# Two last sequences routed by weight to all experts, and squares of the norms written to another tile, in a Mamba and mixture-of-experts kernel

## The chip, the cores and the metric

The kernel runs on one core of one Trainium2 chip. The metric is the device time of one execution, in microseconds (us). Before the change three runs took 5281.4, 5284.5 and 5313.1 us; the median is 5284.5 us. One execution was profiled: it took 5285.57 us, of which 5283.4 us lie between its first and its last instruction (its span).

Five engines have instruction queues of their own and run them in order: TensorE (PE; PEld is its weight load), VectorE (DVE), ScalarE (ACT), GpSimd (POOL) and SyncE (SP), which here only issues DMA transfers.

## What is computed

32 sequences of 512 tokens by 256 channels, all float32, go through one block:

```
h = x + mamba(layernorm(x))                 # in_proj, causal conv of 4 taps, scan over 16 states, gate, out_proj
m = layernorm(h); m = gelu(m @ w1 + b1) @ w2 + b2
x1 = layernorm(x + (h + m))
scores = softmax(x1 @ gate.T)               # 8 experts
weights, idx = top_k(scores, 2)
y_e = (silu(x1 @ wg[e].T) * (x1 @ wu[e].T)) @ wd[e].T        # inner width 128
ffn = sum over the 2 chosen e of weights * y_e  +  the shared expert's y
out = layernorm(x1 + ffn)
```

A token needs only its two experts. A kernel can gather the rows of each expert, or compute every expert for every token and give those not chosen the weight 0.

## The kernel before

Everything about one sequence lies in tiles of 128 partitions: four blocks of 128 tokens (`NC` = 4), or 256 channels as two blocks (`KM` = 2). Four generators describe the work:

- `front(b)`: loads x, takes sums by an ACT copy with an accumulator, `layernorm` (squares on ACT, `nm`, `rs`, `mr` as small POOL operations), transposes through PSUM to `xnT`, in_proj, convolution, the step sizes `dt` and `dt*x`, which go to DRAM (`sdt`, `sdx`) and come back spread over partitions (`dtr`, `dxr`).
- `scan(b)`: 32 steps. In each, `u = dxr * B` (DVE, a few on POOL), two exponentials `pda` on ACT (into two PSUM tiles) and two scans on DVE, then `u = u * C` on POOL, and a PE matmul with `gather` that sums states into `py`. At the end of each quarter `py` is gated by `pz` into `xc`.
- `finish(b)` = `middle(b)` (out_proj `po`, `layernorm`, transposes to `hT`, the MLP `pm`, gelu `hid`) and `back(b)` (`layernorm`, transposes to `x1T`, gate logits `pg`, `route`, the shared expert). `route` finds two experts and their weights per token, counts positions by matmuls, and `back` scatters each token's row twice to `rows_in` in DRAM, 8 indirect DMAs on POOL. The shared expert's result plus x1 goes to DRAM as `sums`.
- `experts(g)`: for a group of sequences, tables on DVE, then blocks of 128 sorted rows, two by two: load rows `xb` and weights `wb` (384 KB), transpose (`pt`, `xT`), gate and up (`pe`), `tb`, `hb`, down (`pd`), `yb` to `rows_out` in DRAM. Then per sequence 8 indirect DMAs on POOL gather `yg`; each is multiplied by a diagonal of weights `dg` into `pc`, added to `sums` as `at`, normalised and written out.

Groups: six of 4 sequences, three of 2, and two of 1 (sequences 30 and 31). A group of n sequences has 8n + 7 blocks: 39, 23 or 15, in all 333. While `scan(b)` runs, `finish(b-1)`, `front(b+1)` and the group's `experts` are called in turn, at set speeds (`N_FRONT`, `N_FINISH`); experts of sequences 28 and 29 run beside `scan(31)`. After the last scan come `finish(31)`, the experts of 30 and those of 31. For the last group of all, `SPACE` gives the tiles of `experts` the buffers that the scan no longer needs.

The order on each engine is not the order of these calls. `Book` records every call; `arrange` (a list scheduler with a cost for each kind of instruction) then picks, among the calls whose inputs and buffers are ready first, the one recorded earliest, and the kernel is emitted in that order. A tile with a tag and `bufs` buffers waits for a buffer of that tag; with one buffer free, only the next tile of the tag in recorded order may take it. `hold` keeps a call behind the one before it, in that order only. Where the scheduler sees PE idle for over 0.6 us while a `py` tile is open, it puts fillers there: matmuls of `zeros` with `ident` into `py`, which add nothing. Each recorded matmul shows as two instructions in the trace (3922 fillers are recorded, 7844 ran).

Squares of a norm (their values are not used, only the sum from the accumulator) go to a tile with the tag `sq`, which has one buffer for all norms of all generators, a new tile for each block of tokens.

Of the kernel before, what the change touches and what calls it, by code (L numbers as in the profile page):

```python
# [122 lines left out]
class Book:  # L123
# [19 lines left out]
    def hold(self):  # L143


        self.held[len(self.calls)] = len(self.calls) - 1
# [213 lines left out]
def kernel(  # L360
# [140 lines left out]
    def totals(nm):  # L501

        return small.tile([P, NC], F32, tag="tot", name=f"tot_{nm}")

    def layernorm(src, tot, nm):

        nm16 = small.tile([P, NC], F32, tag="nm", name=f"nm_{nm}")
        rs = small.tile([P, NC], F32, tag="rs", name=f"rs_{nm}")
        mr = small.tile([P, NC], F32, tag="mr", name=f"mr_{nm}")
        root = DM**0.5  # L510

        nc.gpsimd.tensor_scalar(nm16, tot, -1.0 / (DM * root), 1.0, ALU.mult, ALU.mult)
# [58 lines left out]
    def front(b, got):  # L571
# [107 lines left out]
    dtrs, dxrs, bps, us, bcs = {}, {}, {}, {}, {}  # L679

# [66 lines left out]
    def scan(b):  # L747
# [37 lines left out]
        for k in range(b * per, (b + 1) * per):  # L785
# [33 lines left out]
    def middle(b, ys, got):  # L819
# [9 lines left out]
        mr, rs = layernorm(h, tot, f"b{b}")  # L829
        yield  # L830
        hT = work.tile([P, KM, S], F32, tag="mT", name=f"hT_{b}", bufs=1)
# [72 lines left out]
    def route(b, pg):  # L904
# [3 lines left out]
        g, i0 = place[b]  # L908
# [17 lines left out]
        if i0 == 0:  # L926
# [3 lines left out]
        weight = weights[g][:, i0]  # L930
# [24 lines left out]
        nc.vector.tensor_tensor(both, one, oh, ALU.add)  # L955

# [29 lines left out]
    def back(b, h, tot):  # L986
        mr, rs = layernorm(h, tot, f"c{b}")
        yield
        acc = h
        x1T = work.tile([P, KM, S], F32, tag="mT", name=f"x1T_{b}", bufs=1)  # L990
# [33 lines left out]
        nc.vector.scalar_tensor_tensor(t, pu, 0.5, th, ALU.mult, ALU.mult)  # L1024
        r = rows_in[place[b][0] % 2]
# [22 lines left out]

    def experts(g):

        nb = n_blocks(g)

        last = g == len(groups) - 1

        def space(tag, bufs):
            return SPACE[tag] if last and tag in SPACE else dict(tag=tag, bufs=bufs)

# [92 lines left out]
        for k in range(pairs):  # L1150
# [7 lines left out]
            xT = work.tile([P, KM, 2, P], F32, name=f"xT_{g}_{k}", **space("xT", 2))  # L1158
# [14 lines left out]
            th = work.tile([P, 2, P], F32, name=f"tb_{g}_{k}", **space("tb", 1))  # L1173
            he = work.tile([P, 2, P], F32, name=f"hb_{g}_{k}", **space("hb", 1))
# [10 lines left out]
            yb = work.tile([P, 2, DM], F32, name=f"yb_{g}_{k}", **space("yb", 2))  # L1185
# [7 lines left out]
        for i0, b in enumerate(groups[g]):  # L1193
            at = work.tile([P, NC, DM], F32, tag="at", name=f"at_{b}", bufs=1)
            nc.sync.dma_start(at, sums.pop(b))
            for c0 in range(0, NC, 2):
                po = ps.tile([P, 2, DM], F32, tag="tk", name=f"pc_{b}_{c0}", bufs=4)
                for c in range(c0, c0 + 2):
                    for k in range(TOPK):
                        i = (i0 * TOPK + k) * NC + c  # L1200
                        y = work.tile([P, DM], F32, name=f"yg_{b}_{k}_{c}", **space("yg", 3))
# [8 lines left out]
                        dg = work.tile([P, P], F32, name=f"dg_{b}_{k}_{c}", **space("dg", 2))  # L1210
# [46 lines left out]
    for b in range(NB):  # L1257
# [23 lines left out]
        ending, n_ending = finish(b, fronts[b][1]), N_FINISH  # L1281
# [18 lines left out]
HID_BUFS = 4  # L1300

SPACE = dict(
    wb=dict(tag="u", bufs=U_BUFS),
    xb=dict(tag="dtr", bufs=DT_BUFS),
    xT=dict(tag="bc0", bufs=NG + 1),
    yb=dict(tag="bc1", bufs=NG + 1),
    yg=dict(tag="bc0", bufs=NG + 1),
    dg=dict(tag="dtr", bufs=DT_BUFS),
    tb=dict(tag="hid", bufs=HID_BUFS),
    hb=dict(tag="th", bufs=2),  # L1310
)
# [88 lines left out]
```

## Time and profile before

| what | us |
|---|---|
| median of three runs (all: 5281.4, 5284.5, 5313.1) | 5284.5 |
| profiled execution | 5285.57 |
| its span | 5283.4 |
| PE busy, fillers included | 4831.1 (91%) |
| fillers alone (`py<-ident,zeros`, 7844) | 1002.5 |
| DVE busy | 4165.3 (79%) |
| POOL busy | 3927.9 (74%) |
| ACT busy | 3686.4 (70%) |
| indirect DMAs on POOL, scatter and gather, 256 each | 266.3 and 269.4 |
| end of the last gate of scan 31, from the span's start | 5095.7 |
| from there to the end of the span | 187.7 |

Busy time is the union of an engine's instructions; waiting, branching and issuing of DMAs are not in it. The rows of the profile name instructions by the tiles that they write and read, with numbers left out. Line numbers are of little use here, because nearly every call is made in one place of `Book`; groups are told apart by tiles.

### The profile page before, as it was taken

What the parts mean: (1) busy time and instruction counts of PE and PEld (TensorE: products, weight loads), DVE (VectorE), ACT (ScalarE), POOL (GpSimd) and SP (SyncE); (2) the same over time, 40 slices, a digit from 0 to 9 for tenths busy, and PEclk for the clock granted to TensorE, in tenths of its full rate; (3) what the DMA queues carried; (4) which work ended last, traced back from release to release, by engine and by line L of the source; (5) the groups of instructions that cost most, each with busy time, mean ns of one, the idle gap of its engine ahead of it and who ended that gap; (6) DMA issues with size and microseconds to landing.
All of it is one profiled execution on the core that took longest, in us unless ns stands there. A gap on an engine that the chain in (4) does not pass through costs nothing. (4 is left out here: it accounts for less than half of the span.)

```text
span 5283.4 us, 83847 instructions
## 1 busy us (share of the span) xinstructions
PE 4831.1 (91%) x27968; PEld 2843.5 (54%) x27968; DVE 4165.3 (79%) x5630; ACT 3686.4 (70%) x6812; POOL 3927.9 (74%) x2662
## 2 busy tenths in 40 slices
PE   7999999999999999999999998999998999999885
PEld 3655555555555555555555555555455555655664
DVE  3888888887888878888778887888787768788741
ACT  6677667777767776777777676787776767677542
POOL 3788777778877797777877788777886777777642
PEclk9999999999999999999999999999999999999997
DMA  5753335444454544554444444545356445454534
GB/s 174 242 177 116 109 112 180 150 155 133 144 168 160 162 131 134 168 164 160 146 142 149 162 151 149 170 150 165 124 166 214 157 132 186 143 169 135 170 111 153
DMA packets 521088, 816.68 MB, mean 155 GB/s; under 512 B 49472, under 2 KB 251072, under 8 KB 520656
## 3 DMA queue, kind: packets, MB, share of 16 engines
q1 hardware_dynamic: 493632, 741.95, 43.3%
q0 software_dynamic: 24576, 67.14, 3.9%
q8 instruction: 221, 3.62, 0.3%
q10 hardware_dynamic: 2448, 2.24, 0.1%
q14 instruction: 211, 1.73, 0.1%
HBM read 597.36 MB, written 213.78 MB: 154 GB/s over the span
## 5 line engine op out<-in xcount | busy, mean ns | idle before, releaser
L96 POOL TENSOR_TENSOR u<-u,bc 128x1024 f32<-128x1024 f32 x1024 | 2413.1, 2363 | 597.4 <-DVE u L96 439.3
L96 DVE TENSOR_TENSOR_SCAN u<-pda,u 128x512 f32<-128x512 f32 x2048 | 2400.3, 1209 | 216.1 <-ACT pda L96 187.4
L96 ACT ACTIVATE pda<-dtr,a_neg 128x512 f32<-128x512 f32 x2048 | 1383.6, 686 | 454.1 <-DVE u L96 442.0
L96 DVE TENSOR_TENSOR u<-dxr,bp 128x1024 f32<-128x1024 f32 x896 | 1076.5, 1207 | 191.5 <-PE py L96 77.5
L429 PEld LDWEIGHTS py<-ident,zeros 128*128 128x128 f32 x7844 | 967.8, 197 | 141.0 <-issue 128.4
L429 PE MATMUL py<-ident,zeros 128*128 128x128 f32 x7844 | 1002.5, 281 | 0.0
L96 PE MATMUL py<-u,gather 128*32 128x512 f32 x4096 | 650.9, 623 | 40.6 <-POOL u L96 40.3
L96 PE MATMUL pin<-xpad,taps 32*32 32x512 f32 x4096 | 465.7, 590 | 10.5 <-POOL xpad L96 7.6
L96 PEld LDWEIGHTS pe<-xT,wb 128*128 128x128 f32 x2664 | 358.5, 208 | 171.2 <-DMA wb<-in_w_e_dram 55.9
L96 PE MATMUL pe<-xT,wb 128*128 128x128 f32 x2664 | 386.9, 297 | 69.1 <-DMA wb<-in_w_e_dram 55.1
L96 POOL DMA_INDIRECT rows_in<-h,idx x256 | 266.3, 1040 | 184.6 <-DMA rows_in<-h,idx 99.7
L96 ACT COPY bp<-bc 128x512 f32<-128x512 f32 x512 | 299.6, 585 | 119.7 <-DVE u L96 104.0
L96 POOL DMA_INDIRECT yg<-rows_out,got x256 | 269.4, 1052 | 141.6 <-issue 67.5
L96 ACT ACT_TABLE_LOAD x279 | 358.0, 1283 | 14.4 <-DMA in_sb<-in_in_w_dram 7.9
L96 POOL TENSOR_TENSOR u<-dxr,bc 128x1024 f32<-128x1024 f32 x128 | 302.3, 2362 | 51.2 <-DMA dxr<-sdx 41.0
L96 PE MATMUL po<-out_sb,xc 128*128 128x256 f32 x1024 | 272.9, 402 | 26.8 <-DVE xc L96 26.0
L96 PEld LDWEIGHTS pin<-xpad,taps 32*32 32x32 f32 x4096 | 119.5, 104 | 313.1 <-issue 273.5
L96 PE MATMUL pz<-xnT,in_sb 128*128 128x512 f32 x512 | 267.8, 635 | 10.7 <-DVE h L96 9.0
L96 PEld LDWEIGHTS po<-out_sb,xc 128*128 128x128 f32 x1024 | 187.9, 196 | 139.1 <-DVE xc L96 54.1
L96 PE MATMUL pm<-w_sb,hid 128*128 128x256 f32 x1024 | 255.8, 390 | 1.0 <-ACT hid L96 0.5
L96 PE MATMUL pin<-xnT,in_sb 128*128 128x512 f32 x512 | 252.2, 612 | 3.3 <-DVE h L96 1.8
L96 PEld LDWEIGHTS py<-u,gather 128*32 128x32 f32 x4096 | 100.3, 110 | 278.8 <-POOL u L96 127.7
(168 smaller groups left out, 6388.9 us busy)
## 6 DMA issues: line engine op xcount, KB each, us to landing
dtr<-sdt SPq DMA_DIRECT2D x512, 256.0 KB, 3.6
dxr<-sdx SPq DMA_DIRECT2D x512, 256.0 KB, 3.4
wb<-in_w_e_dram SPq DMA_DIRECT2D x333, 384.0 KB, 3.8
bc<-rows SPq DMA_DIRECT2D x256, 256.0 KB, 3.4
xb<-rows_in SPq DMA_DIRECT2D x333, 128.0 KB, 2.5
rows_out<-yb SPq DMA_DIRECT2D x161, 256.0 KB, 4.4
sdt<-dt SPq DMA_DIRECT2D x64, 512.0 KB, 3.2
sdx<-dtx SPq DMA_DIRECT2D x64, 512.0 KB, 3.8
```

Of the source, the lines that this page charges most:

```text
L96: lambda: getattr(getattr(self.book.nc, self.name), op)(*map(made, a), **{k: made(v) for k, v in kw.items()})
L429: nc.warm = lambda t: nc.nc.tensor.matmul(t[:, :P], zeros.make(), ident.make(), start=False, stop=False)
```

## The change

It has two parts.

First, sequences 30 and 31 (`ALONE` = 2) are in no group. For them `route` stops after the choice and multiplies scores by the choice: `every` holds, for each token, the weight of each of the 8 experts, 0 for six of them. The position matmuls, the index arithmetic, the 8 scatters, `sums`, the tables, 15 blocks and the 8 gathers of each are gone. In their place `by_all` computes each expert for all 512 tokens from `x1T`, as the shared expert is computed: gate and up (`ag`, `au`, four matmuls of 128x512), tanh, two DVE products, down (`ad`, four matmuls of 128x256), and four DVE operations that add `ad` times the weight to the sum `acc`. Weights are loaded whole, 384 KB an expert: for sequence 30 into the `wb` buffers, which the experts of 28 and 29 use at the same time; for 31 into the eight `u` buffers of the scan, held in the schedule behind the last scan instruction. `SPACE` goes. `finish(30)` is called in 65 pieces (`N_ALONE`) in place of 41, beside `scan(31)`.

Second, the squares of the norms a, b and c (and the copies in `front`) go to the first 256 columns of the tile that later takes the norm's transposed result: `xnT` (two buffers), `hT` or `x1T` (one buffer, tag `mT`, for both). So that tile is claimed before the squares and not after them. The norm d, at the end, keeps `sq`, one tile for its four squares.

```diff
-    def hold(self):
...
-        self.held[len(self.calls)] = len(self.calls) - 1
+    def hold(self, call=-1):
...
+        n = len(self.calls)
+        self.held[n] = n - 1 if call < 0 else call
...
-    def layernorm(src, tot, nm):
+    def layernorm(src, tot, nm, sq=None):
...
         nc.gpsimd.tensor_scalar(nm16, tot, -1.0 / (DM * root), 1.0, ALU.mult, ALU.mult)
         for c in range(NC):
-            sq = work.tile([P, DM], F32, tag="sq", name=f"sq_{nm}_{c}", bufs=1)
+            if sq is None:
+                sq = work.tile([P, DM], F32, tag="sq", name=f"sq_{nm}", bufs=1)
             nc.scalar.activation(
                 sq,
                 src[:, c, :],
...
         tot = totals(f"a{b}")
+        xnT = work.tile([P, KM, S], F32, tag="xnT", name=f"xnT_{b}")
+        sq = xnT[:, 0, :DM]
         for c in range(NC):
-            sq = work.tile([P, DM], F32, tag="sq", name=f"cp_{b}_{c}", bufs=1)
             nc.scalar.activation(sq, xt[:, c, :], AF.Identity, accum_out=tot[:, c : c + 1])
-        mr, rs = layernorm(xt, tot, f"a{b}")
-        yield
-        xnT = work.tile([P, KM, S], F32, tag="xnT", name=f"xnT_{b}")
+        mr, rs = layernorm(xt, tot, f"a{b}", sq)
+        yield
...
+            if k == len(steps) - 1:
+                scanned.append(len(nc.calls) - 1)
...
             add(h[:, c, :], xt[:, c, :], po[:, :DM], tot[:, c : c + 1])
-        mr, rs = layernorm(h, tot, f"b{b}")
-        yield
         hT = work.tile([P, KM, S], F32, tag="mT", name=f"hT_{b}", bufs=1)
+        mr, rs = layernorm(h, tot, f"b{b}", hT[:, 0, :DM])
+        yield
...
     while NB - sum(sizes) > 2 * GROUP:
         sizes.append(GROUP)
-    while NB - sum(sizes) > 2:
+    while NB - sum(sizes) > ALONE:
         sizes.append(GROUP // 2)
-    sizes += [1] * (NB - sum(sizes))
...
         n = NC * E
-        g, i0 = place[b]
+        alone = b not in place
...
-        if i0 == 0:
+        if alone:
+            weight = tl("own", [P, TOPK, NC], bufs=1)
+        else:
+            g, i0 = place[b]
+        if not alone and i0 == 0:
             slots[g] = tl("slots", [P, len(groups[g]), TOPK, NC], bufs=3)
             weights[g] = tl("weights", [P, len(groups[g]), TOPK, NC], bufs=3)
             carries[g] = first
-        weight = weights[g][:, i0]
+        if not alone:
+            weight = weights[g][:, i0]
...
         both = tl("both", wide)
         nc.vector.tensor_tensor(both, one, oh, ALU.add)
+        if alone:
+
+            every = tl("every", wide, bufs=1)
+            nc.vector.tensor_tensor(every, both, sc, ALU.mult)
+            return every
...
     def back(b, h, tot):
-        mr, rs = layernorm(h, tot, f"c{b}")
+        x1T = work.tile([P, KM, S], F32, tag="mT", name=f"x1T_{b}", bufs=1)
+        mr, rs = layernorm(h, tot, f"c{b}", x1T[:, 0, :DM])
         yield
         acc = h
-        x1T = work.tile([P, KM, S], F32, tag="mT", name=f"x1T_{b}", bufs=1)
...
         nc.vector.scalar_tensor_tensor(th, th, 1.0, pg, ALU.add, ALU.mult)
         nc.vector.scalar_tensor_tensor(t, pu, 0.5, th, ALU.mult, ALU.mult)
+        if b not in place:
+            yield from by_all(b, h, x1T, idx, t, wd)
+            return
...
+    def all_weights(b):
+
+        own = LAST if b == NB - 1 else dict(tag="wb", bufs=3)
+        for e in range(E):
+            w = work.tile([P, NW], F32, name=f"wa_{b}_{e}", **own)
+            nc.hold(*(scanned if b == NB - 1 else ()))
+            nc.sync.dma_start(w, w_e[e * P : (e + 1) * P, :])
+            yield w
+
+    def by_all(b, h, x1T, every, t, wd):
+
+        acc = h
+        if b < NB - 1:
+            acc = xin.tile([P, NC, DM], F32, tag="x", name=f"acc_{b}")
+        for c0 in range(0, NC, 2):
+            po = ps.tile([P, 2, DM], F32, tag="tk", name=f"ps_{b}_{c0}", bufs=4)
+            for i in range(2):
+                tokens(po[:, i, :], [t], wd.unsqueeze(1), c0 + i)
+            yield
+            cs = slice(c0, c0 + 2)
+            nc.vector.tensor_tensor(acc[:, cs, :], h[:, cs, :], po, ALU.add)
+        ws = iter(alone.pop(b)) if b in alone else all_weights(b)
+        after = next(ws)
+        tot = totals(f"d{b}")
+        for e in range(E):
+            w, after = after, next(ws, None)
+            wg, wu, wd = parts(w)
+            tag = dict(tag="pda") if b == NB - 1 and e % 2 else dict(tag="tk", bufs=4)
+            pg = ps.tile([P, S], F32, name=f"ag_{b}_{e}", **tag)
+            pu = ps.tile([P, S], F32, name=f"au_{b}_{e}", **tag)
+            channels(pg, wg, slice(0, P), x1T)
+            channels(pu, wu, slice(0, P), x1T)
+            yield
+            th = work.tile([P, S], F32, tag="th", name=f"tha_{b}_{e}", bufs=2)
+            nc.scalar.activation(th, pg, AF.Tanh, scale=0.5)
+            t = work.tile([P, S], F32, tag="hid", name=f"ha_{b}_{e}", bufs=HID_BUFS)
+            nc.vector.scalar_tensor_tensor(th, th, 1.0, pg, ALU.add, ALU.mult)
+            nc.vector.scalar_tensor_tensor(t, pu, 0.5, th, ALU.mult, ALU.mult)
+            yield
+            for c0 in range(0, NC, 2):
+                po = ps.tile([P, 2, DM], F32, tag="tk", name=f"ad_{b}_{e}_{c0}", bufs=4)
+                for i in range(2):
+                    tokens(po[:, i, :], [t], wd.unsqueeze(1), c0 + i)
+                yield
+                for i in range(2):
+                    c = c0 + i
+                    sum_of = dict(accum_out=tot[:, c : c + 1]) if e == E - 1 else {}
+                    nc.vector.scalar_tensor_tensor(
+                        acc[:, c, :],
+                        po[:, i, :],
+                        every[:, c, e : e + 1],
+                        acc[:, c, :],
+                        ALU.mult,
+                        ALU.add,
+                        **sum_of,
+                    )
+        mr, rs = layernorm(acc, tot, f"d{b}")
+        yield
+        for c in range(NC):
+            normalize(acc[:, c, :], acc[:, c, :], mr, rs, c)
+        nc.sync.dma_start(out[b].rearrange("(c p) d -> p c d", p=P), acc)
...
-                x = work.tile([P, DM], F32, name=f"xb_{g}_{i}", **space("xb", 3))
+                x = work.tile([P, DM], F32, name=f"xb_{g}_{i}", tag="xb", bufs=3)
...
-                w = work.tile([P, NW], F32, name=f"wb_{g}_{i}", **space("wb", 3))
+                w = work.tile([P, NW], F32, name=f"wb_{g}_{i}", tag="wb", bufs=3)
...
-    fronts, mids, sums = {}, {}, {}
+    fronts, mids, sums, alone = {}, {}, {}, {}
 
     def finish(b, ys):
+        if b == NB - 1:
+            alone[b] = list(all_weights(b))
         yield from middle(b, ys, mids)
         yield from back(b, *mids.pop(b))
...
-        ending, n_ending = finish(b, fronts[b][1]), N_FINISH
+        ending = finish(b, fronts[b][1])
+        n_ending = N_FINISH if b in place else N_ALONE
...
-
-SPACE = dict(
-    wb=dict(tag="u", bufs=U_BUFS),
-    xb=dict(tag="dtr", bufs=DT_BUFS),
...
+ALONE = 2
+N_ALONE = 65
+
+LAST = dict(tag="u", bufs=U_BUFS)
```

The other places of `experts` that used `space` get their own tags and buffers back in the same way.

More of the change, by code (lines that the diff above doesn't have):

```diff
@@ L679 @@
     dtrs, dxrs, bps, us, bcs = {}, {}, {}, {}, {}
+    scanned = []
     def load(i):
@@ L828, in middle @@
             add(h[:, c, :], xt[:, c, :], po[:, :DM], tot[:, c : c + 1])
-        mr, rs = layernorm(h, tot, f"b{b}")
+        hT = work.tile([P, KM, S], F32, tag="mT", name=f"hT_{b}", bufs=1)
+        mr, rs = layernorm(h, tot, f"b{b}", hT[:, 0, :DM])
         yield
-        hT = work.tile([P, KM, S], F32, tag="mT", name=f"hT_{b}", bufs=1)
         def get(c):
@@ L1049, in experts @@
     def experts(g):
         nb = n_blocks(g)
-        last = g == len(groups) - 1
-        def space(tag, bufs):
-            return SPACE[tag] if last and tag in SPACE else dict(tag=tag, bufs=bufs)
         def tl(nm, shape, dtype=F32):
@@ L1157, in experts @@
                     nc.tensor.transpose(pt[:, q, i, :], x[:, q * P : (q + 1) * P], ident)
-            xT = work.tile([P, KM, 2, P], F32, name=f"xT_{g}_{k}", **space("xT", 2))
+            xT = work.tile([P, KM, 2, P], F32, name=f"xT_{g}_{k}", tag="xT", bufs=2)
             nc.scalar.copy(xT[:, :, :n, :], pt[:, :, :n, :])
@@ L1172, in experts @@
             yield
-            th = work.tile([P, 2, P], F32, name=f"tb_{g}_{k}", **space("tb", 1))
-            he = work.tile([P, 2, P], F32, name=f"hb_{g}_{k}", **space("hb", 1))
+            th = work.tile([P, 2, P], F32, name=f"tb_{g}_{k}", tag="tb", bufs=1)
+            he = work.tile([P, 2, P], F32, name=f"hb_{g}_{k}", tag="hb", bufs=1)
             pg, pu, th_, he_ = pm[:, 0, :n], pm[:, 1, :n], th[:, :n], he[:, :n]
@@ L1184, in experts @@
                 )
-            yb = work.tile([P, 2, DM], F32, name=f"yb_{g}_{k}", **space("yb", 2))
+            yb = work.tile([P, 2, DM], F32, name=f"yb_{g}_{k}", tag="yb", bufs=2)
             nc.scalar.copy(yb[:, :n], po[:, :n])
@@ L1200, in experts @@
                         i = (i0 * TOPK + k) * NC + c
-                        y = work.tile([P, DM], F32, name=f"yg_{b}_{k}_{c}", **space("yg", 3))
+                        y = work.tile([P, DM], F32, name=f"yg_{b}_{k}_{c}", tag="yg", bufs=3)
                         nc.gpsimd.indirect_dma_start(
@@ L1209, in experts @@
                         )
-                        dg = work.tile([P, P], F32, name=f"dg_{b}_{k}_{c}", **space("dg", 2))
+                        dg = work.tile([P, P], F32, name=f"dg_{b}_{k}_{c}", tag="dg", bufs=2)
                         nc.scalar.mul(dg, ident, weights[g][:, i0, k, c : c + 1])
@@ L1300 @@
 HID_BUFS = 4
-SPACE = dict(
-    wb=dict(tag="u", bufs=U_BUFS),
-    xb=dict(tag="dtr", bufs=DT_BUFS),
[L1305 to L1311, printed above, removed]
+ALONE = 2
+N_ALONE = 65
+LAST = dict(tag="u", bufs=U_BUFS)
 _OUTS = [((32, 512, 256), "float32")]
```

## The prediction

> **What bounds the kernel now.** I read busy time by stretch first. A four-sequence period in mid-kernel (1855.0 to 2480.2) takes 625.2 us; a trace query gives DVE 516.27 us of it (83%), POOL 491.00, ACT 456.70, PE 575.98. No engine is full; PE looks so because it is fed fillers. The second answer is that of the fillers alone.
>
> ```profile
> 1855.00:2480.20 625.20, 111.28 (x848) 106.78 (x848) 0.00 (x0) 0.97 0.47 153
> ...
> 4918.50:5095.70 177.20, 33.87 (x258) 32.74 (x258) 0.00 (x0) 0.92 0.48 151
> ```
>
> Columns: stretch, length, PE busy, PEld busy, POOL busy, granted clock, DMA share, GB/s. A filler costs 111.28/848 = 0.131 us. The end is different. Stretches of it, with PE, PEld, DVE, ACT, POOL, clock:
>
> ```profile
> 4918.50:5072.00 153.50, 132.53 (x752) 90.35 (x752) 125.52 (x190) 84.54 (x158) 97.28 (x63) 0.92 0.51 160
> 5072.00:5095.00 23.00, 20.08 (x133) 15.94 (x134) 2.21 (x10) 9.06 (x26) 18.71 (x18) 0.93 0.30 92
> ...
> 5131.00:5200.00 69.00, 42.52 (x206) 34.81 (x205) 16.86 (x65) 18.07 (x42) 9.56 (x12) 0.76 0.60 185
> 5200.00:5254.00 54.00, 35.38 (x192) 28.09 (x191) 8.05 (x24) 17.50 (x42) 9.97 (x13) 0.90 0.50 156
> ```
>
> DVE finishes its scans at 5072; POOL needs 23 us more. Then come 188 us in which nothing is busy for long. The timelines of the engines (start, length, what) and the chain of waits say why:
>
> ```profile
> 5087.89 4.67 POOL L96 TENSOR_TENSOR u<-u,bc 128x1024 f32<-128x1024 f32 x2
> ...
> 5115.30 7.15 PE L96 MATMUL pm<-hT,w_sb 128*128 128x512 f32 x16
> 5122.28 7.07 PE L96 MATMUL pm<-w_sb,hid 128*128 128x256 f32 x32
> ...
> 5167.04 3.35 PE L96 MATMUL pe<-xT,wb 128*128 128x128 f32 x16
> ...
> 5240.03 2.05 PE L96 MATMUL pe<-xT,wb 128*128 128x128 f32 x16 [0.68 <-ACT xT L96]
> ...
> 5256.47 1.17 POOL L96 DMA_INDIRECT yg<-rows_out,got  x1 [34.72 <-DMA rows_out<-yb]
> 5257.94 1.01 POOL L96 DMA_INDIRECT yg<-rows_out,got  x1 [0.30 <-issue]
> ```
>
> ```profile
> 5253.86 1.69 DMA rows_out<-yb
> ...
> 5268.80 1.21 PE pc L96 x2
> ...
> 5276.45 0.98 ACT at L96 x2
> ```
>
> The end is a chain: MLP, routing, 8 scatters (5152 to 5180), load rows, 15 blocks in pairs (a pair every 4 to 6 us, though its PE work is some 4), DRAM, 8 gathers of 1.32 us, last sums, norm. I call the last `gather` matmul of scan 31, at 5094.9, G; the span ends at G + 188.5.
>
> **The last sequence alone.** In the built kernel's PE order nothing else is left after G but experts 5 to 7 of sequence 30, the last block of 28 and 29, their 16 gathers, and sequence 31. Step by step from G:
>
> (1) To the start of `pm` (20.4 us before, 5115.3). `pd` of the last block comes after the rest of `po`, and gate and up of expert 5. A dense 128x512 row costs 7.15/16 = 0.447 us and a 128x256 row 7.07/32 = 0.221; an expert has 8 of each, 3.58 + 1.77 = 5.34 us. So `pd` ends about 2.4 + 3.6 + 0.9 = 7 after G. In SP's order six of the eight weight loads of 31 stand before `wb` of that last block, and the two others before more of 30's: the held loads are released together as scan 31 ends. At the 361 GB/s that the stretch from 150 to 160 reached, 6 x 0.393 MB are 6.5 us, half of it under the scan's last steps: +3. The Trainium skill, "DMA: Bandwidth & Descriptors", section "Queues, rings and completion order", says that each DMA engine takes descriptors in ring order; by that rule the whole 6.5 us would be paid, 3.5 us more; no row here tells. From the end of `pd` to the first gather 3.3 (5253.2 to 5256.5): G + 13.3. Sixteen gathers at 1.34 make 21.4, and the small POOL operations that now stand among and behind them (three norms: 1.65 each from `rs` to `mr`, and single ones) 6: `mr` of the norm b is ready at G + 40.7, and normalise, transpose, copy to `hT` add 4.3 (0.6 + 4 x 0.5 + 1.45 and hand-overs). G + 45. The new wait of these squares, for `mT`, which `x1T` of 30 holds until its last `au`, ends at about G + 25 and is covered by POOL's queue of gathers; without that cover nothing changes before G + 30.
>
> (2) `pm` to the last add: 5115.30 to 5129.82, 14.5, the same. (3) To `x1T`: 10.4 before, less 1.1 of ACT copies `yb` and `xT` between: 9.3.
>
> (4) Gate 1.96, shared expert 5.35, eight experts 42.7, dense: 50. DVE's 2 x 0.69 + 4 x 0.42 = 3.1 us and ACT's 0.6 an expert lie beside PE; routing (5.6 us, 5142.0 to 5147.6) lies beside the first experts. One stall at the last expert: 1. (5) From the last `pc` (5269.99) to the end: 13.4, the same.
>
> Sum: 45 + 14.5 + 9.3 + 51 + 13.4 = 133 in place of 188.5: -55 us. Bounds: -45 (the burst wholly paid, gathers slowed by three buffers) to -62 (step 1 at 38).
>
> **Sequence 30 beside scan 31.** Added before G: experts 0 to 4, 5 x 5.34 = 26.7 us of PE and 15 of DVE. Moved behind G: 16 `pc` (7.0). Removed: position matmuls (2.1), 8 scatters on POOL (about 1.25 each, 10). In scan 31 PE had 119.4 us of real work; now 137. Its fillers are counted in the orders: 129 before, 76 now, 33.9 to 19.9 us. With PE idle between 8 (as in sequence 30) and 24 (as in 31) the stretch takes 165 to 181 us, against 177. By DVE: scans ended 153.6 after the start; +15 is 169, then 3.4 for POOL's last product and its matmul, as POOL's 18.71 us after DVE's end were mostly gathers, now behind G: 172. I take -6. Ends: -11, and +27 if all five experts add to the length.
>
> **Squares.** Each of the three tiles is taken earlier: `xnT` must wait for the last `pz` two sequences back, where copies had no such wait; in the new ACT order the copies stand just behind the tanh of that same `pz`, so nothing queued behind (the exponentials of the scan) waits more. The one-buffer tag tied all norms to one recorded order and let one other instruction in between any two squares; that goes. Of 32 norms b, the four squares stand in one run in 31 (before: 1). Such a run takes 2.5 us (5099.38 to 5101.88), where first to last took 3.7 in the median.
>
> Does a run hold up DVE? I sorted the 2,047 exponentials of the trace by the ACT instructions since the one before and took DVE's idle time before its scan: 0 or 1: under 0.04 us, 3: 0.24, 4: 0.29, 5: 0.48, 6 to 8: 0.23 to 0.28. With the new order's counts (94 fewer of three, 45 more of five, 20 more of six to eight) that changes by +4 us in all: nothing. The last product of `front` (`dtx`) stands nine steps later in sum over 31 sequences, still six steps (29 us) ahead of the first `u` that needs it, and the two DMAs take 7.4: covered.
>
> What speaks for a gain: over scans 0 to 30 the new PE order has 167 fillers fewer, 334 instructions, 43.8 us. A period of four has 394 for 424. That is time only where the rest gets shorter too; short gaps get no filler. Bounds -44 and, for a loss, +33 (65 more runs of five and more at 0.5). I take a third, -15.
>
> Table loads: 279 to 287, 8 x 1.28 = 10 us of ACT, among 30% idle: nothing.
>
> **Sum.** 5285.6 (the profiled execution, 1.1 above the median) - 55 - 6 - 15 = 5210 us.
>
> **Rivals.** (a) The fillers' whole 44 us come off: 5181. For: in mid-kernel, periods with equal counts differ by 1% at most. Against: PE does not pace these stretches. (b) Sequence 30 does not fit beside scan 31: PSUM banks (four, tag `tk`) and three `wb` buffers serve two strands, +27, and the squares bring nothing: 5286 + 27 - 55 = 5258. For: PE already waits for `wb` in that stretch. (c) The two sequences' work is there but clocked low: the same 16 rows took 3.35 us at 5167 and 2.05 at 5240, with granted clock 0.76 and 0.90 around. All of step 4 at 3.35/2.05 costs 32 more, and the change does not give what it says: 5242. The Trainium skill, "TensorE: Matmul & The Clock Gate", Part 1, says that an idle window of about 3.4 us halves the clock and a busy one restores it; by that rule only the first 3.4 us of step 4 are slow, which speaks against (c), and 0.76 fits a PE that goes idle often. (d) Slower: the runs of squares starve DVE. There are 4 runs a sequence (copies, a, b, c), 124 in all; 1.8 us of each (three squares and reads) is new in one piece. If DVE paid it all: 5286 + 223 - 61 = 5448. It decides for slower by 1% from 0.92 us a run. Against it: the sorted idle times, 0.48 us at most.
>
> **Chances.** Forecast 0.50, (a) 0.16, (b) 0.21, (c) 0.05, (d) 0.08. Range: (a) with -11 and -62 gives 5168, (b) with -45 gives 5268; rounded outwards 5160 to 5272, which leaves out (d) and the rims of (a) and (b). Under 1%, about 53 us, this measurement tells no change. Faster by over 1% (below 5232): forecast and (a), 0.66; within 1%: (b) and (c), 0.26; slower: 0.08.
>
> **What would show it.** Right: `pm` of 31 starts some 45 us after the last `gather`, eight experts follow at 5.3 us each without PE idle, the end comes at G + 133; G lies 165 to 181 us after the end of scan 30; a period of four takes 615 to 625 us. Wrong: PE waits for `wa` or for PSUM between experts; the 16 gathers start over 20 us after G; scan 31 takes over 195; a period takes over 630, with DVE waiting for `pda` longer than 187 us (this trace's total).

## The result and the profile after

Six runs of the changed kernel took 5219.83 to 5242.21 us, median 5225.45; six runs of the kernel before, the three of the table of before among them, took 5281.4 to 5324.42, median 5304.41. The ratio is 0.9858, with a 95% interval from 0.9836 to 0.9881: 1.4% faster, some 75 us. (The three new runs of the kernel before were slower than the three that the prediction started from; 5210 of 5285.6 is a ratio of 0.9857.) The profiled execution took 5219.83 us, its span is 5218.1.

First the stretches of the profile after, in the columns of the first fence of the prediction but for all instructions: length, then PE, PEld, DVE, ACT and POOL busy, granted clock, DMA share, GB/s. Sequences 12 to 15 are the first line, scan 31 the second.

```profile
1851.00:2475.00 624.00, 574.70 (x3274) 322.70 (x3272) 520.17 (x690) 462.78 (x841) 491.42 (x330) 0.98 0.47 153
4921.40:5083.30 161.90, 148.94 (x800) 95.82 (x801) 136.23 (x205) 88.51 (x154) 87.85 (x46) 0.97 0.51 162
```

The same two stretches for the fillers alone (length, PE, PEld and POOL busy, clock, DMA):

```profile
1851.00:2475.00 624.00, 99.06 (x788) 95.32 (x788) 0.00 (x0) 0.98 0.47 153
4921.40:5083.30 161.90, 19.93 (x152) 19.12 (x152) 0.00 (x0) 0.97 0.51 162
```

A period has 60 filler instructions fewer than before, 12 us of PE, and is 1 us shorter (625.2 to 624.0). Scan 31 is 15 us shorter (177.2 to 161.9): POOL is rid of scatters and gathers there (116.0 to 87.9 us), DVE has 8 us more, and G now lies at 5082.5. After G, first POOL's timeline:

```profile
5076.29 2.35 POOL L96 TENSOR_TENSOR u<-u,bc 128x1024 f32<-128x1024 f32 x1 [0.67 <-DVE u L96]
5092.84 1.17 POOL L96 DMA_INDIRECT yg<-rows_out,got  x1 [14.20 <-issue]
...
5116.83 1.01 POOL L96 DMA_INDIRECT yg<-rows_out,got  x1 [0.31 <-issue]
...
5122.33 0.20 POOL L96 TENSOR_TENSOR mr_b<-mr_b,rs_b 128x4 f32<-128x4 f32 x1
```

and PE's:

```profile
5123.51 1.18 PE L96 MATMUL tp_b<-ident,nrmB 128*128 128x128 f32 x4 [1.53 <-ACT nrmB L96]
...
5126.79 8.80 PE L96 MATMUL pm<-hT,w_sb 128*128 128x512 f32 x16 [0.66 <-ACT hT L96]
5135.43 7.07 PE L96 MATMUL pm<-w_sb,hid 128*128 128x256 f32 x32
5148.21 2.17 PE L96 MATMUL tp_c<-ident,h 128*128 128x128 f32 x8 [5.71 <-ACT h L96]
...
5153.13 2.99 PE L96 MATMUL pg<-gt_sb,x1T 128*128 128x8 f32 x14
...
5157.82 5.13 PE L96 MATMUL ag<-x1T,wa 128*128 128x512 f32 x8
...
5177.51 1.99 PE L96 MATMUL ad<-wa,ha 128*128 128x256 f32 x8
...
5204.27 1.99 PE L96 MATMUL ad<-wa,ha 128*128 128x256 f32 x8 [0.79 <-DVE ha L96]
```

Where the end before was a chain of blocks, DRAM and gathers, it is now gathers of other sequences up to `pm`, the MLP, and 55 us of experts in which PE is hardly idle: the five rounds from 5177.51 to 5204.27 take 5.35 us each. From G to the span's end it is 135.6 us, before 188.5.

### The profile page after: what moved, and what is told of

Same layout as the page of the kernel before. It is cut to its first block, busy times and chain, and to the rows that moved or that the text cites. A ratio compares the mean times of both kernels' runs of the same rounds, so it can differ in the third digit from the quotient of the medians.

```text
span 5218.1 us, 82267 instructions
## 1 busy us (share of the span) xinstructions
PE 4811.2 (92%) x27360; PEld 2767.9 (53%) x27360; DVE 4199.7 (80%) x5628; ACT 3718.3 (71%) x6770; POOL 3898.5 (75%) x2628
## 5 line engine op out<-in xcount | busy, mean ns | idle before, releaser
L430 PEld LDWEIGHTS py<-ident,zeros 128*128 128x128 f32 x7404 | 906.5, 196 | 115.9 <-issue 106.0
L430 PE MATMUL py<-ident,zeros 128*128 128x128 f32 x7404 | 938.6, 281 | 0.0
L96 PE MATMUL py<-u,gather 128*32 128x512 f32 x4096 | 663.9, 627 | 42.9 <-POOL u L96 42.3
L96 PEld LDWEIGHTS pe<-xT,wb 128*128 128x128 f32 x2424 | 317.0, 205 | 140.4 <-issue 38.4
L96 PE MATMUL pe<-xT,wb 128*128 128x128 f32 x2424 | 341.6, 294 | 51.2 <-DMA wb<-in_w_e_dram 32.5
L96 ACT COPY bp<-bc 128x512 f32<-128x512 f32 x512 | 299.7, 585 | 100.4 <-DVE u L96 94.1
L96 POOL DMA_INDIRECT rows_in<-h,idx x240 | 250.6, 1044 | 159.6 <-DMA rows_in<-h,idx 103.3
L96 POOL DMA_INDIRECT yg<-rows_out,got x240 | 254.1, 1059 | 99.5 <-issue 61.0
```

Of the source, the lines that this page charges most:

```text
L96: lambda: getattr(getattr(self.book.nc, self.name), op)(*map(made, a), **{k: made(v) for k, v in kw.items()})
L430: nc.warm = lambda t: nc.nc.tensor.matmul(t[:, :P], zeros.make(), ident.make(), start=False, stop=False)
```

## The experiments

Twelve runs follow, in three batches: ten other kernels, the changed kernel a second time (after_again) and one of the ten a second time (untied_again). Those of a batch ran on one chip, beside runs of the kernel before. Profiled executions of one kernel on two chips differ (the changed kernel: 5218.1 and 5252.6 us), so differences under 1% are read from the ratios, and the profiles tell where things stand within the end. The stretch from the end of scan 30 to the end of the span hardly moves between such executions (296.7 and 297.3), so this table splits each difference of medians: what that stretch, read from one profiled execution, differs from 364.9 us of before, and the rest, which is then put down to scans 0 to 30. The ratios' intervals reach 0.14 to 0.35% to each side, 8 to 19 us.

| kernel | ratio to before, 95% interval | medians, difference | end stretch | its difference | scans 0 to 30 |
|---|---|---|---|---|---|
| changed kernel | 0.9858 [0.9836, 0.9881] | -79.0 | 296.7 | -68.2 | -11 |
| after_again (the same) | 0.9871 [0.9842, 0.9899] | -69.2 | 297.3 | -67.6 | -2 |
| alone_only | 0.9900 [0.9882, 0.9918] | -62.0 | 304.3 | -60.6 | -1 |
| squares_only | 0.9998 [0.9976, 1.002] | -0.9 | 363.0 | -1.9 | +1 |
| squares_run | 1.0066 [1.0043, 1.0088] | +26.9 | 366.8 | +1.9 | +25 |
| squares_untied | 0.9909 [0.9894, 0.9923] | -48.4 | 367.8 | +2.9 | -51 |
| no_fill | 0.9883 [0.9855, 0.991] | -69.7 | 299.7 | -65.2 | -4 |
| after_untied | 0.9797 [0.9762, 0.9831] | -106.7 | 296.0 | -68.9 | -38 |
| untied_again (the same) | 0.9784 [0.9765, 0.9803] | -118.9 | 296.0 | -68.9 | -50 |
| gathers_behind | 0.9846 [0.9813, 0.9878] | -93.0 | 284.0 | -80.9 | -12 |
| gathers_own | 0.9835 [0.9802, 0.9869] | -83.3 | 288.7 | -76.2 | -7 |
| untied_behind | 0.9769 [0.975, 0.9787] | -124.9 | 284.5 | -80.4 | -44 |
| alone_four | 0.9944 [0.9924, 0.9964] | -26.9 | 293.2 | -71.7 | +45 |

### The two parts alone

**alone_only** is the changed kernel with the squares of before:

```diff
-        mr, rs = layernorm(h, tot, f"b{b}", hT[:, 0, :DM])
+        mr, rs = layernorm(h, tot, f"b{b}")
...
-                sq = work.tile([P, DM], F32, tag="sq", name=f"sq_{nm}", bufs=1)
+            sq = work.tile([P, DM], F32, tag="sq", name=f"sq_{nm}_{c}", bufs=1)
```

> Only the first part: sequences 30 and 31 by weight to all experts; squares as before the change, in the one-buffer tag sq. Theory E (the whole gain is the end: 68 us of the 65 us shorter span come after scan 30 ends, -15 in scan 31 and -53 behind it, +3 before): ratio to the kernel before 0.985 to 0.989, scans 0 to 30 within 5 us of 4918.5, end of scan 30 to the end of the span about 297 us as in the changed kernel. Rival Q (the squares' move is a good part of the gain, by unblocking norms in the end): ratio above 0.991 and the stretch behind scan 30 longer than 310 us.

Measured: 0.9900, and an end of 304.3 us, a little beyond theory E (0.989, 297) and short of rival Q (0.991, 310). Scans 0 to 30 are as before. So the two sequences by weights bring nearly the whole gain; the 7.6 us that the end is longer than in the changed kernel belong to the squares. The timeline of ACT shows why:

```profile
5124.44 0.51 ACT L96 ACTIVATE sq_d<-at,nm_d 128x256 f32<-128x256 f32 x1
5124.85 0.19 ACT L96 ACTIVATION_READ_ACCUMULATOR sq_d<-at,nm_d 128x1 f32 x1
5125.07 0.51 ACT L96 ACTIVATE sq_b<-h,nm_b 128x256 f32<-128x256 f32 x1
```

and PE's what came of it:

```profile
5132.26 1.18 PE L96 MATMUL tp_b<-ident,nrmB 128*128 128x128 f32 x4 [13.32 <-ACT nrmB L96]
```

The one-buffer `sq` ties the norm b of sequence 31 behind the norms d of the sequences whose gathers come first: `sq_b` starts when the last `sq_d` has been read, and PE stands 13.3 us before `tp_b` (1.5 in the changed kernel, in its PE rows above). This is a use of the second part at the one place where it lies on the path.

**squares_only** is the kernel before with the second part alone (each norm's squares go to `xnT`, `hT` or `x1T`, as in the diff of the change).

> Only the second part: squares and copies go to the tiles of the transposed results; all 32 sequences in groups as before. Theory E: no measurable change, ratio 0.997 to 1.003, although the PE order has 304 fewer fillers executed and DVE waits for pda some 150 us more than the 187 us of before; other waits of DVE (for py, bp, pg) fall by as much. Rival F (the forecast's term: fewer fillers are time): ratio 0.991 to 0.997. Rival D (runs of squares starve DVE): ratio above 1.003.

Measured: 0.9998. Nothing, as theory E had it, though the trace has 304 filler instructions fewer than before, 40 us of PE at 0.131 us each, and DVE waits 349.8 us for `pda` in place of 187.4.

**squares_run** is the kernel before with one tile `sq` for a norm in place of one for each block of tokens. The tie to the other norms stays; in the trace ACT now has 95 runs of exactly four squares or copies, before 7 (in the changed kernel 106).

```diff
-            sq = work.tile([P, DM], F32, tag="sq", name=f"sq_{nm}_{c}", bufs=1)
+            if c == 0:
+                sq = work.tile([P, DM], F32, tag="sq", name=f"sq_{nm}", bufs=1)
```

> The kernel before with one sq tile for the four squares (or copies) of a norm in place of four: runs of squares as in the changed kernel for the norms b (31 of 32 in one run), but norms stay tied to one order by the one buffer and no tile is claimed earlier. Theory E: ratio 0.996 to 1.004, DVE's waits for pda rise above 230 us. Rival D: above 1.004. If squares_only differs from this one by over 0.4%, the tie between norms or the earlier claim matters by itself.

Measured: 1.0066, slower, as rival D had it: 25 to 35 us. The second part of the change, with as many runs, costs nothing (squares_only), so it must give as much back elsewhere. This edit alone does not tell runs from another cause: with one tile for a norm, the one buffer is also held for four squares at a time, which makes the tie coarser.

### Untying without runs

Two things changed at once for the squares: they are no longer tied by one buffer, and they stand in runs. **squares_untied** does only the first, on the kernel before: the squares keep a tile for each block (439 squares or copies stand singly in ACT's order in the trace; before 449, in the changed kernel 57), but the norms b and c have one tag and a and d another. The tiles are bf16 so that they fit; a square takes ACT the same time (500 to 502 ns in the mean, by norm; before 500 to 503).

```diff
-            sq = work.tile([P, DM], F32, tag="sq", name=f"sq_{nm}_{c}", bufs=1)
+            sq = work.tile([P, DM], mybir.dt.bfloat16, tag="sq1" if nm[0] in "bc" else "sq0", name=f"sq_{nm}_{c}", bufs=1)
...
-            sq = work.tile([P, DM], F32, tag="sq", name=f"cp_{b}_{c}", bufs=1)
+            sq = work.tile([P, DM], mybir.dt.bfloat16, tag="sq0", name=f"cp_{b}_{c}", bufs=1)
```

**after_untied** does the same in the changed kernel, in place of its tiles `xnT`, `hT`, `x1T`; **untied_again** is that kernel in another batch.

> The changed kernel, but the squares go to scratch tiles of their own again (bf16, so that they fit): one one-buffer tag for the norms b and c, another for a and d, a tile for each block. So the squares of b and c are no longer tied to those of a and d, and they still stand singly in ScalarE's order (482 single ones against 64). Nothing else of the changed kernel is undone. Theory T: runs of four squares starve VectorE's exponentials (squares_run: +0.7%), and the untying gives about as much back; with one and without the other the kernel is 0.3 to 0.8% faster than the changed kernel: ratio to before 0.978 to 0.983, VectorE's wait for pda back from 339 to about 190 us. Rival N: VectorE's waits only trade places (what pda loses, py, bp and u give back), and what squares_run lost came from the tie itself: ratio 0.984 to 0.988 as the changed kernel, with pda at 190 us and the other waits up. In both, the stretch from the end of the gate of scan 31 stays 133 to 138 us, since norm b of 31 is not behind norm d.

> The kernel before, with the untied single squares of after_untied alone (bf16 scratch, one tag for the norms b and c, one for a and d) and no sequence by weights. Theory T (the tie of the one-buffer tag cost time, and the changed kernel gave the gain back by runs of four squares): 0.990 to 0.996 of before, the same 0.4 to 0.9% that after_untied has over the changed kernel (0.9797 against 0.9871), all of it before the end of scan 30. Rival N (the untying is worth nothing by itself; after_untied's lead is one between orders that differ by chance): 0.998 to 1.002. The stretch from the gate of scan 31 to the end stays 185 to 197 us in both, as in before.

> after_untied a second time, on whatever chip this is, since its lead over the changed kernel (0.9797 [0.9762, 0.9831] against 0.9871 [0.9842, 0.9899]) rests on one batch: 0.977 to 0.983 if the lead is real, 0.984 to 0.988 if it was the batch.

Measured: 0.9797 and 0.9784 for the changed kernel so altered, and 0.9909 for the kernel before so altered, whose end is not shorter. The times of theory T came, on two chips and from two starting points: the tie cost 0.9%, and runs of four cost about 0.7% (squares_run against before; the changed kernel against after_untied, 0.9871 to 0.9797, agrees, and there the squares also take the tiles `xnT`, `hT` and `x1T` earlier). Runs are all that the two comparisons have in common; no kernel has runs alone. In the change the one pays for the other: -0.9% and +0.7% leave -0.2%, which lies within the interval of squares_only (0.9976 to 1.002).

One number of the expectation did not come: VectorE's wait for `pda` did not go back to 190 us (281.1 in after_untied, 279.7 in squares_untied). DVE's groups (busy, mean ns, then idle time before them and what ended most of it), before:

```profile
L96 DVE TENSOR_TENSOR_SCAN u<-pda,u 128x512 f32<-128x512 f32 x2048 | 2400.3, 1209 | 216.1 <-ACT pda L96 187.4 <-POOL u L96 26.4
L96 DVE TENSOR_TENSOR u<-dxr,bp 128x1024 f32<-128x1024 f32 x896 | 1076.5, 1207 | 191.5 <-PE py L96 77.5 <-ACT bp L96 69.8 <-issue 22.2
```

in the changed kernel:

```profile
L96 DVE TENSOR_TENSOR_SCAN u<-pda,u 128x512 f32<-128x512 f32 x2048 | 2403.8, 1210 | 352.2 <-ACT pda L96 336.1 <-POOL u L96 9.6 <-ACT dg L96 3.0
L96 DVE TENSOR_TENSOR u<-dxr,bp 128x1024 f32<-128x1024 f32 x896 | 1077.2, 1207 | 118.5 <-PE py L96 46.8 <-ACT bp L96 38.8 <-issue 15.2
```

and in squares_untied:

```profile
L96 DVE TENSOR_TENSOR_SCAN u<-pda,u 128x512 f32<-128x512 f32 x2048 | 2401.7, 1208 | 296.7 <-ACT pda L96 279.7 <-POOL u L96 13.3 <-issue 0.7
L96 DVE TENSOR_TENSOR u<-dxr,bp 128x1024 f32<-128x1024 f32 x896 | 1075.0, 1205 | 130.4 <-PE py L96 35.2 <-POOL u L96 32.2 <-ACT bp L96 30.4
```

The waits trade places: with the tie gone DVE waits longer for its exponentials and less for `py` and `bp`, whether the squares stand in runs or not; without runs the first is 56 us smaller. So this one wait does not account for the times: in squares_untied it is 92 us longer than before, and the kernel is 48 us faster. Which chain of front or finish became shorter by the untying is not settled by these traces.

### Fillers

**no_fill** is the changed kernel without fillers:

```diff
-    nc.warmed = "py"
+    nc.warmed = None
```

> The changed kernel without any filler on PE (7404 fewer executed); the order is otherwise the same. Theory E (a filler stands in a gap of PE, it is no time): not faster than the changed kernel; PE's granted clock falls below 0.9 and matmuls get longer, so some per cent slower than it. Rival F: a third of 7404 x 0.131 us, 320 us, comes off: ratio near 0.92.

Measured: 0.9883, not faster than the changed kernel (0.9858 and 0.9871), at a lower granted clock (span and mean granted clock, of this kernel and then of the changed one):

```profile
core 0: 5243.4 us, clock 0.886
```

```profile
core 0: 5218.1 us, clock 0.961
```

With all 7404 fillers gone (938.6 us of PE) the time is 0.1 to 0.3% longer, which the intervals do not tell from nothing. Rival F (0.92) falls. Theory E was right that it is not faster and that the clock falls below 0.9; the loss of some per cent that it went on to forecast did not come. A filler lies in time that PE has to spare, and a smaller count of them tells nothing of a gain.

### The stretch before `pm`

**gathers_behind** is the changed kernel with the 16 gathers of sequences 28 and 29 called behind the MLP of 31; the experts of 28 and 29 are called somewhat faster beside scan 31 (`pace` 1.22), so that their blocks are done by then:

```diff
+        pace = 1
+        if b == NB - 1:
+            now, pace = n_late - 15, 1.22
...
-            (late, now, 1),
+            (late, now, pace),
...
-    run(ending)
+    for i, _ in enumerate(ending):
+        if i >= 14:
+            next(late, None)
     run(late)
```

> The changed kernel with the 16 gathers and sums of sequences 28 and 29 recorded behind the MLP of sequence 31, so that they run beside its MLP and its first experts. Theory P (the prediction's step 1): the 16 gathers on GpSimd hold up norm b of 31. Then pm of 31 starts at about G+26 in place of G+44 (what is left is the wait for the tile mT, which x1T of 30 frees at its last au, some 17 to 20 us after G, and the norm behind it), nothing else is longer, and the kernel is 14 to 20 us faster than the changed one: ratio to before 0.981 to 0.984. Rival Q: the gathers only move on: their sums stand before tp_c in TensorE's order, and so the gate of 31 begins no earlier than before: no gain, 0.985 to 0.988.

Measured: 0.9846, between the ranges of P and Q, with an interval that reaches into both and takes in the changed kernel of the same batch (0.9871). The ratio does not decide; the trace does. In its timelines of POOL and PE

```profile
5110.26 0.19 POOL L96 TENSOR_SCALAR nm_b<-tot_b 128x4 f32<-128x4 f32 x1 [2.09 <-DVE h L96]
...
5124.56 1.17 POOL L96 DMA_INDIRECT yg<-rows_out,got  x1 [0.16 <-issue]
```

```profile
5120.95 8.75 PE L96 MATMUL pm<-hT,w_sb 128*128 128x512 f32 x16 [0.66 <-ACT hT L96]
```

`pm` starts 22.8 us after G (5098.1), in place of 44.3, and the first gather comes behind it. So the queue of gathers on POOL did hold up norm b, as step (1) of the prediction had it. From the gate of scan 31 to the end it is 117.6 us in place of 134.8; scan 31 takes back 4.5 (166.4, with PE at 136.8 us of real work in place of 129.0). Together that is 12.7 us, a little under the 14 to 20 of theory P. Rival Q falls: what stands behind `pm` moves forward with it.

**gathers_own** is that, with `hT` and `x1T` of sequence 31 in the tag `xnT`, so that they need not wait for `x1T` of 30:

```diff
-        hT = work.tile([P, KM, S], F32, tag="mT", name=f"hT_{b}", bufs=1)
+        own = dict(tag="xnT", bufs=2) if b == NB - 1 else dict(tag="mT", bufs=1)
+        hT = work.tile([P, KM, S], F32, name=f"hT_{b}", **own)
```

> gathers_behind, and hT and x1T of sequence 31 in the tag xnT (which has no tenant left by then) in place of mT, so that the norm b of 31 has no wait for x1T of 30. The prediction said that this wait is covered by the queue of gathers; here that cover is gone. Theory P: pm of 31 starts at G+15 to G+19, another 7 to 10 us earlier than gathers_behind, ratio to before 0.979 to 0.983; experts 5 to 7 of sequence 30 then run beside or before it on TensorE. Rival R: TensorE's own order (po, the experts of 30, pd) sets pm, and the tile wait costs nothing: the same as gathers_behind within 3 us in the profile.

Measured: 0.9835, the same as gathers_behind, and `pm` again at G + 22.8 (5160.65, G at 5137.8), so rival R is right. From PE and POOL:

```profile
5146.22 3.19 PE L96 MATMUL po<-out_sb,xc 128*128 128x256 f32 x14
```

```profile
5149.95 0.19 POOL L96 TENSOR_SCALAR nm_b<-tot_b 128x4 f32<-128x4 f32 x1 [2.09 <-DVE h L96]
```

The wait for `mT`, which the prediction covered by the gathers, costs nothing even without that cover: `po` ends behind experts of sequence 30 at G + 11.6, and norm b starts at G + 12.1 in both kernels. By the prediction nothing changes before G + 30 without the cover; `pm` came 7 us ahead of that.

### Two further versions

**untied_behind** is after_untied and gathers_behind together.

> after_untied and gathers_behind together. If both gains are what they seem, they add: after_untied's 0.9797 less some 14 us of gathers_behind (rest after the gate of scan 31 117.6 in place of 132.9, scan 31 three longer) gives 0.976 to 0.979. Rival: the order with untied squares has its gathers nearly clear already, or the squares of the norms d of 28 and 29, tied to nothing in after_untied's end, come back in the way: 0.979 to 0.983.

Measured: 0.9769, as expected and the lowest ratio of all, 2.3% below the kernel before. Its end (284.5) is as short as that of gathers_behind. The step from untied_again (0.9784 in the same batch) is inside the intervals: the end of the trace shows both gains together, the time alone does not tell.

**alone_four** is the changed kernel with `ALONE = 4`: sequences 28 to 31 go by weights, and only 30 keeps a tile `acc` of its own. (The groups are then six of four and two of two; the expectation's last full group of four does not arise.)

```diff
-        if b < NB - 1:
+        if b == NB - 2:
             acc = xin.tile([P, NC, DM], F32, tag="x", name=f"acc_{b}")
...
-ALONE = 2
+ALONE = 4
```

> The changed kernel with four sequences by weights (28 to 31) in place of two: the last group by sorted rows is then a full one of four. Theory U (each sequence by weights costs TensorE 43 us less its share of the blocks, beside a scan that has 48 us of fillers or 20): sequences 28 and 29 fit beside scans 29 and 30, and what is left behind G is no gather, so pm of 31 starts at G+15 to 20: rest after the gate of 31 some 112 to 118 us, scans 29 to 31 together 0 to 15 us longer than in the changed kernel: ratio 0.980 to 0.988. Rival V: with VectorE some 21 us of sums more in each of scans 29 and 30 and TensorE at 140 us of real work or more, those scans take 165 to 185 us each and eat the gain: 0.988 to 0.996.

Measured: 0.9944, slower than the changed kernel by 0.7 to 0.9%. The ratio is that of rival V, but not by its sizes, 165 to 185 us for each of scans 29 and 30. Stretches (columns as in the first fence) of scans 29, 30 and 31:

```profile
4623.70:4785.30 161.60, 151.71 (x878) 87.14 (x879) 133.57 (x183) 107.75 (x188) 107.75 (x66) 0.99 0.42 135
4785.30:5006.40 221.10, 198.85 (x909) 107.15 (x908) 154.72 (x222) 116.19 (x201) 104.15 (x63) 0.92 0.37 117
5006.40:5168.40 162.00, 141.36 (x682) 86.50 (x681) 136.90 (x197) 91.52 (x177) 109.75 (x77) 0.92 0.32 102
```

Scan 29 takes 161.6 us, in the changed kernel 156.6; scan 30 takes 221.1, in the changed kernel 170.9. PE has 198.9 us of work beside scan 30, only 14.5 of them fillers, and ten experts of sequences 28 and 29 fall there (40 rows `au`, 4 an expert). What a sequence by weights saves is the end, and only the last ones stand there; the others are 43 us of PE each, with no chain to cut. One or three sequences, or another pace of the calls, were not tried. Nor does theory U's other half come: with no gather left behind G, `pm` starts at G + 40.4 (5208.05, G at 5167.6), since experts 4 to 7 of sequence 30 stand before it on PE.

## Why the prediction was right, point by point

**The sum.** 76 us were forecast; the medians differ by 79.0 and 69.2. By parts the traces give -53 for the stretch behind G (forecast -55), -15 for scan 31 (-6), and what is left of the medians is -11 and -2 for scans 0 to 30 (-15). So the largest term is right for its reasons, and that the sum came so near is in part luck: 9 us more in scan 31 stand in for what the squares did not bring.

**The last sequence alone** (-55). Right, step by step. From G to the end 135.6 us, predicted 133. First gather at G + 10.3 (13.3), `mr` of norm b at G + 40.0 (40.7; the gathers with what stands among them took 29.7 us in place of 27.4), `pm` at G + 44.3 (45), MLP to the gate of 31 another 24.1 (14.5 + 9.3), step (4) 55.3 (51), the last step 12.0 (13.4). The +3 for the burst of weights did not come: seven weight loads are issued from 5067.9 to 5074.3, the load of the last `wb` at 5079.2, and the matmuls that read it start at 5083.4. The rule that the prediction cites from the Trainium skill, "DMA: Bandwidth & Descriptors", section "Queues, rings and completion order", by which it would have paid all of its 6.5 us, was therefore not put to the test: the burst stood 4.9 us ahead of the transfer that it was to delay.

Step (4)'s excess of 4.3 us is of the size that the clock cost. Windows of a few us, in the columns of the first fence:

```profile
5148.20:5152.00 3.80, 3.33 (x11) 2.08 (x12) 0.00 (x0) 2.51 (x5) 0.00 (x0) 0.50 0.02 4
...
5156.00:5160.00 4.00, 4.00 (x6) 1.80 (x7) 1.92 (x10) 1.49 (x2) 0.00 (x0) 0.50 0.00 0
5160.00:5164.00 4.00, 4.00 (x9) 1.67 (x8) 2.23 (x9) 0.60 (x1) 0.00 (x0) 0.89 0.00 0
5164.00:5168.00 4.00, 4.00 (x11) 1.76 (x10) 1.70 (x3) 0.88 (x2) 0.00 (x0) 1.00 0.00 0
```

The third number from the end is the granted clock: 0.50 from the restart of PE at 5148.2 (5.71 us idle before) until about 5160.9 (a mean of 0.89 over four us is 0.88 us at 0.50 and the rest at 1.00), then 1.00 to the last expert. Some 10 us of step (4) at half speed are 5 us lost. So rival (c), all of step (4) slow, fell. The Trainium skill ("TensorE: Matmul & The Clock Gate", Part 1) says that an idle window of about 3.4 us halves the clock and that a busy one of that length restores it. The trace agrees with the halving. For the restoring it matters from which row one counts. From PE's first row it took 12.7 us; but up to 5156 these rows are transposes `tp_c`, gate logits `pg` of eight columns and two rows of `pu`, and from the rows of 128x512 that then follow without a gap (5155.98) it took 4.9. The MLP of the same trace, behind pauses of 3.4 and 1.5 us, has such rows at once:

```profile
5126.80:5130.20 3.40, 3.40 (x4) 1.50 (x5) 0.00 (x0) 2.58 (x8) 3.24 (x4) 0.50 0.00 0
5130.20:5135.40 5.20, 5.20 (x13) 2.28 (x12) 0.00 (x0) 5.17 (x10) 1.88 (x4) 1.00 0.01 2
```

There the clock is 0.50 for the first 3.4 us of `pm` and 1.00 after it; in gathers_behind for the first 3.3 us of `pm` (5120.95 to 5124.2), in alone_only for the first 6.2 (5135.5 to 5141.7). So counted from dense rows of 128x512 the clock came back in 3.3 to 6.2 us, which is the rule's figure or up to twice that. What the prediction missed is that step (4) opens with 5 us in which most rows are narrow, and that the clock stayed at half through them; whether rows of eight columns count as idle no run tests.

**Sequence 30 beside scan 31** (-6, ends -11 and +27). Scan 31 came out 15 us shorter, beyond the better end. PE's real work there rose to 129.0 us (predicted 137), and POOL's last product starts as soon as DVE's last `u` is there (5076.29, in the POOL rows above), with no gathers of experts in its queue. Not all of the 15 us need be due to that: kernels that leave sequence 30 in its group also have scan 31 at 167.1 to 171.1 us (squares_only, squares_run, squares_untied; before 177.2), with 8 to 9 us more behind it. How the gain divides between scan 31 and what follows thus depends on the order; the sum of both, 68 us, is firm. Rival (b) fell.

**Squares and fillers** (-15). Here a term was mis-sized, and so was what it hid. The step reads "I take a third, -15", a third of 44 us of fillers. Fillers are not time: squares_only executes 304 fewer with a ratio of 0.9998, no_fill none at all. By the table scans 0 to 30 are 2 to 11 us shorter in the changed kernel, with an uncertainty of 12 to 15; so -15 is not excluded, but the reason was wrong. In its place the runs show two terms that nearly cancel. The step "that changes by +4 us in all: nothing" priced the runs of squares by idle times that the kernel before showed; squares_run says +25 to +35 us. DVE's wait for `pda` rose from 187.4 to 339.3 us, which the prediction had named as a sign of being wrong, and a period still took 624 us, because the untying, which "that goes" left without a price, is worth -48 us (squares_untied). Sorted idle times of the old order did not give the price of a new order: intervals with 7 ACT instructions between two exponentials, 0.23 us of DVE idle time each before (58 of them), cost 1.10 us each after (61). Why they cost little before is not shown; it may be that the old order put long gaps where they did no harm.

**Rivals.** (a), fillers worth their 44 us, fell by no_fill and squares_only. (c) fell with step (4), above. (d), the runs of squares, was right that they cost time, but squares_run gives 0.3 to 0.4 us for each of the 88 runs that it has more than the kernel before, not the 0.92 from which it decides.

## What to carry to other kernels

What the end of a kernel costs is a chain, and it can be summed row by row before the run; a cheaper route that costs more work is worth it for the items whose chain ends the kernel (here two sequences gained, four lost most of it again). A scratch tile that nobody reads can still tie unrelated work together through its one buffer: giving two pairs of norms a buffer each was worth 0.9% here, and setting the instructions in runs of four between those that feed the busiest engine cost about 0.7%. Counts of filler matmuls were no measure of time.

## What the runs showed of the hardware

- After pauses of 5.7 us (changed kernel, before `tp_c`) and 13.3 us (alone_only, before `tp_b`) TensorE ran at half its clock for 12.7 and 9.4 us from its first row, and for 4.9 and 6.2 us from where rows of 128x512 followed each other without a gap. Sixteen rows of 128x512 took 7.15 us before and 7.03 in untied_behind, at a clock of 1.00, 8.80 in the changed kernel and 10.20 in alone_only. That fits: 3.4 and 6.2 us at half speed are 1.7 and 3.1 us lost.
- Without fillers the mean granted clock fell from 0.961 to 0.886, and the ratio to the kernel before is 0.1 to 0.3% above that of the changed kernel, within the intervals: a twelfth of TensorE's clock cost next to nothing in this kernel.
- The write type of a square (float32 or bf16) made no difference on ScalarE: 500 to 503 ns for 128x256 before, 500 to 502 in squares_untied.
